# Moving a step's convolution taps ahead of the state sums in the periods that also project B and C

## The chip, the cores and the metric

The kernel runs on one core of one Trainium2 chip. The metric is the time of one execution on the device in microseconds (us); the time given for a kernel is the median of several runs. The core has engines that run side by side, each with its own queue of instructions: TensorE (PE in the profile, with its weight loads as PEld), VectorE (DVE), ScalarE (ACT), GpSimd (POOL) and SyncE (SP, which here issues the DMAs). An engine works its queue in the order in which the program issued it.

## The reference, cut to what matters

The reference is two layers on an input of 2 x 512 x 512: a feed-forward block with 4-bit weights, a state-space block (Mamba-2), the feed-forward block again, then a memory block, an attention block and the memory block again. The change is in the state-space block only. Cut to what matters there (128 heads of 64, 8 groups with a state of 128, chunks of 128 positions):

```python
proj = einsum('bsd,od->bso', h, in_proj_w)          # gate, hBC, dt
hBC = silu(causal_conv(hBC, conv_w, conv_b))         # 4 taps along the sequence
hid, B, C = split(hBC)
dt = softplus(dt + dt_bias); A = -exp(A_log)
M = einsum('bcihn,bcjhn->bcijh', Ch, Bh) * L         # L: decay inside a chunk
Y_diag = einsum('bcijh,bcjhp->bcihp', M, hc)         # hc = hid * dt
states = einsum('bclhn,bhcl,bclhp->bchpn', Bh, decay_states, hc)
prev_states = recurrence(states)                     # over the 4 chunks
Y_off = einsum('bclhn,bchpn,bhcl->bclhp', Ch, prev_states, exp(A_cs))
y = Y_diag + Y_off + Dp * hid
yg = y * silu(gate)
out = residual + group_rms_norm(yg) @ out_proj_w.T
```

## The kernel before, in words

The state-space block is `Kernel.ssm`, from L523. Its work is cut into 128 steps: for each of 8 groups, for each of 2 batches, 8 pairs of heads (`PAIRS`). One step handles one tile of 128 channels (two heads) over the 512 positions of a batch. The loop calls `period(n)` (L837) for n from 0 to 129, and each period works on three steps at once: `cur` (step n) gets its projections, its decay matrices and its convolution; `p1` (step n-1) gets its states and its output `y`; `p2` (step n-2) is multiplied with the output weights and added up.

The whole loop runs under a manual schedule: each engine gets its instructions in exactly the order in which `period` issues them. A tile that is written on one engine and read on another brings a wait. PSUM, the memory that TensorE writes to, is cut into eight banks (L528): "tr" 1, "po" 4, "dd" 1, "mm" 1 and "y" 1. Each name but "po" has a single buffer, so the next tile of that name waits until all readers of the last one are done.

In a period TensorE does, in this order: the projection of the step's channels `cp_h` (bank "dd", L715); the state matmuls `st` of p1 (bank "tr", L908); the output product `po` of p2 (L832); the two parts of `py` of p1 (bank "y"), first those from the decay matrices M (L989), then those from the states (L998); the gate projection `pg` (bank "mm"); and the transposes `ht` of the convolved channels `hid` (bank "tr", L1042).

VectorE does: `hc` and the gate's silu `v` for p1; two scans that build the decay matrices M of cur (`within`, L795; the scan is L806); the state sums `st` of p1 over the chunks (L918); the step's own taps, three per convolution (`conv_taps`, L727, the taps are L729); the product of M with CB (`times_c`, L814, L820); `hid` (the silu, L738); and `yg` of p1 (L1005, L1009).

ScalarE does: the Tanh of the gate (L849); six scalings `hd` that feed the state matmuls (L861); the Exp of the first M (L811); the first tap of the convolution, out of PSUM into `acc` (`first_tap`, L720, L724); the copy of the first chunk's state out of PSUM (L913), on which the state sums wait; the Exp of the second M (L955); and the Tanh at the end of `conv_taps` (L734).

Two periods out of eight carry more. When q is 5 (`PAIRS - 3`) the B of the next batch or group is projected, when q is 6 its C, unless there is no next one. That makes 30 periods of the 128. `group_b` and `group_c` (L767, L770) put the projection on TensorE right behind `cp_h`, into the "mm" bank (the one that `pg` takes later in the period), and append three functions to the list `late`: the first tap on ScalarE, the taps (VectorE, then a Tanh on ScalarE) and the silu at the end. `period` calls them at three places: the first tap after the state copy, the taps after the step's own taps, and the silu after `yg`. In the C periods the transposes `bt` (L777) and their copy `Btok` (L779) come as well, in the bank "tr". In periods 1 to 7 the setup of the second batch's decays (`setup_later`, L694) is spread over the period, also in the bank "tr".

Of the kernel before, what the change touches and what calls it, by code (L numbers as in the profile page):

```python
# [77 lines left out]
class Kernel:  # L78
# [758 lines left out]
    def period(self, n):  # L837
# [4 lines left out]
        late = []  # L842
# [24 lines left out]
        if cur is not None:  # L867
            g, b, q = cur.g, cur.b, cur.q
            sh = self.sh[g, b]
            for ot in (OT_HID + cur.ct, cur.ct):  # L870
                self.group_w(ot, b)
            p = self.project(self.gw[OT_HID + cur.ct], b, f"cp_h{cur.n}", "dd")
            after = cur.after()
            if after is not None and q == PAIRS - 3:
                self.group_b(*after, late)
            if after is not None and q == PAIRS - 2:
                self.group_c(*after, late)

            if n == 1:
                self.within(p1)  # L880
                nc.scalar.activation(p1.M[1], p1.M[1], AF.Exp)
                self.times_c(p1)
            if n > 0:
                self.within(cur)
            if n == 0:

                cur.pg = self.project(self.gw[cur.ct], b, f"pg{cur.n}")
                self.start(NT - 1)
            if n != 1:
                conv = self.first_tap(p, cur.ct, f"h{cur.n}")  # L890
            if n == 0:
                th = self.conv_taps(*conv)
                self.group_bt(0, 0)
                self.turn(NT - 1, "po")
                self.group_cb(0, 0, "po")
# [28 lines left out]
        if n == 1:  # L924
            conv = self.first_tap(p, cur.ct, f"h{cur.n}")
# [27 lines left out]
        if cur is not None:  # L953
            if n > 0:
                nc.scalar.activation(cur.M[1], cur.M[1], AF.Exp)  # L955
                self.setup_later(n, 1)
                th = self.conv_taps(*conv)
            for one in late:
                one[1]()
            if n > 0:  # L960
                self.times_c(cur)
            cur.hid = sp.tile([P, S], F32, tag="hid", name=f"hid{cur.n}", bufs=2)
            self.silu(cur.hid, th, conv[2])
# [817 lines left out]
```

## Time and profile before

| what | value |
|---|---|
| time, median of 3 runs | 2813.09 us |
| the three runs | 2813.09, 2822.13, 2789.83 us |
| the profiled execution, its own time | 2795.29 us |
| its span in the trace | 2793.5 us |
| its mean granted TensorE clock | 0.982 |
| busy share of PE, DVE, ACT, POOL | 96%, 73%, 39%, 19% |
| PE busy between 300 and 2300 us | 1977.6 us of 2000 |

How to read it: the profile comes from one execution, so sums are made against that execution's own time, which lies below the median. In lines of groups the fields are the line of the program, the engine, the operation, what it writes and reads (out<-in), the shapes and the count. In the timeline the first two columns are the start in us from the start of the span and the length in us of a merged run of equal instructions; a bracket at the end gives how long the engine had been idle before and what released it. In the view of waits the three numbers are the sum in us, the count and the longest. A wait labelled "issue" is one in which the profile shows nothing that the engine waited for. The ends of matmuls are modelled, and a mean over equal lines hides single ones.

### The profile page before, as it was taken

Reading aid. Unit: us, or ns where it says so; the run is one execution under the profiler, and the core shown is the slowest. Engines: PE = TensorE matmul, PEld = TensorE weight load, DVE = VectorE, ACT = ScalarE, POOL = GpSimd, SP = SyncE. Lnnn points to the kernel's source line nnn. Section 1 sums busy time; section 2 is a strip of 40 time slices with the busy share of each in tenths; the row PEclk is TensorE's granted clock in tenths of the full one; section 3 lists DMA queues with packets and bytes.
Section 4 is the critical chain, followed back from the end, with each engine's and each line's share of the span. In section 5 each row is a group of like instructions: output and inputs, shape, how many; then the busy total and the mean of one; then the engine's idle time right before and its main releaser. Section 6 shows DMA issues by size and latency. Waiting matters only on the chain.

```text
span 2793.5 us, 33412 instructions
## 1 busy us (share of the span) xinstructions
PE 2689.8 (96%) x12208; PEld 1398.5 (50%) x12208; DVE 2030.9 (73%) x3632; ACT 1102.6 (39%) x2411; POOL 522.1 (19%) x344
## 2 busy tenths in 40 slices
PE   8999999999999999999999999999999999788887
PEld 4444555555555555555555555555554444444443
DVE  7836877877888788787888878878886533555545
ACT  2214443544444344344443444434443212244442
POOL 0001131313313123132321322313230000110000
PEclk9999999999999999999999999999999999889996
DMA  7623133223223322322322332232121020000000
GB/s 209 198 89 113 72 107 128 87 91 123 96 83 124 113 72 103 129 87 80 126 105 83 121 105 80 106 128 87 68 99 46 27 84 1 0 1 1 1 1 31
DMA packets 75621, 237.77 MB, mean 85 GB/s; under 512 B 9825, under 2 KB 10401, under 8 KB 58945
## 3 DMA queue, kind: packets, MB, share of 16 engines
q1 hardware_dynamic: 70416, 226.00, 23.2%
q10 hardware_dynamic: 4752, 8.65, 0.8%
q8 instruction: 97, 1.59, 0.2%
q0 software_dynamic: 288, 0.98, 0.1%
q14 instruction: 68, 0.55, 0.1%
HBM read 223.80 MB, written 11.80 MB: 84 GB/s over the span
## 4 chain that ended last, share of the span: by engine, by line
PE 85%; DVE 9%; ACT 4%; issue 1%; DMA 0%; ACTq 0%; SPq 0%; DVEq 0%
PE pg L715 15%; PE po L832 14%; PE cp_h L715 14%; PE fo L501 5%; PE fmm L334 5%; PE py L989 4%; PE st L908 3%; PE fy L334 2%; DVE acc_h L729 2%; PE py L998 2%; PE cp_BT L715 2%; PE cp_CT L715 2%; PE ht L1042 2%; PE w L1553 1%; PE pqk L1425 1%; PE fdd L334 1%
## 5 line engine op out<-in xcount | busy, mean ns | idle before, releaser
L715 PE MATMUL pg<-hT_s,wi 128*128 128x512 f32 x1024 | 472.5, 604 | 14.4 <-issue 6.9
L832 PE MATMUL po<-wo,yg 128*128 128x512 f32 x1024 | 460.7, 593 | 0.5 <-DVE yg L1009 0.5
L715 PE MATMUL cp_h<-hT_s,wi 128*128 128x512 f32 x1024 | 460.6, 592 | 0.0
L806 DVE TENSOR_TENSOR_SCAN M<-rows,later 128x512 f32<-128x512 f32 x256 | 457.8, 1827 | 0.0
L1016 POOL TENSOR_TENSOR ssum<-ssum,sq 128x512 f32<-128x512 f32 x112 | 142.2, 1270 | 1233.0 <-ACT sq L1015 1233.0
L715 PEld LDWEIGHTS pg<-hT_s,wi 128*128 128x128 f32 x1024 | 184.2, 189 | 221.6 <-issue 213.4
L729 DVE SCALAR_TENSOR_TENSOR acc_h<-cp_h,small,acc_h 128x511 f32<-128x511 f32 (+2 forms) x384 | 286.1, 745 | 9.0
L832 PEld LDWEIGHTS po<-wo,yg 128*128 128x128 f32 x1024 | 184.8, 190 | 184.4 <-issue 183.6
L715 PEld LDWEIGHTS cp_h<-hT_s,wi 128*128 128x128 f32 x1024 | 184.6, 190 | 183.6 <-issue 183.6
L822 POOL TENSOR_TENSOR Cs<-CT,rows 128x768 f32<-128x768 f32 x128 | 251.9, 1968 | 17.6 <-PE py L998 15.7
L918 DVE SCALAR_TENSOR_TENSOR st<-st,whole,st 128x64 f32<-128x64 f32 x512 | 108.8, 274 | 125.7 <-ACT st L913 125.7
L734 ACT ACTIVATE th_h<-acc_h 128x512 f32<-128x512 f32 x128 | 80.5, 629 | 292.2 <-DVE acc_h L729 286.5
L861 ACT ACTIVATE hd<-ht,end 128x64 f32<-128x64 f32 x768 | 170.4, 323 | 35.8 <-DVE hc L853 35.7
L1015 ACT ACTIVATE sq<-yg 128x512 f32<-128x512 f32 x112 | 70.6, 630 | 286.9 <-DVE yg L1009 286.9
L820 DVE TENSOR_TENSOR M<-M,CB 128x512 f32<-128x512 f32 x256 | 164.4, 683 | 0.1
L811 ACT ACTIVATE M<-M 128x512 f32<-128x512 f32 x128 | 80.7, 630 | 199.1 <-DVE M L806 199.1
L853 DVE TENSOR_TENSOR hc<-ht,dt 128x512 f32<-128x512 f32 x128 | 88.0, 688 | 86.2 <-PE ht L1042 86.2
L1517 DVE CUSTOM_DVE_ANT_0 j<-s,future 128x384 f32<-128x384 f32 (+3 forms) x256 | 112.8, 486 | 48.8 <-PE s L1507 48.6
L989 PEld LDWEIGHTS py<-M,hc 128*64 128x64 f32 x2048 | 109.4, 136 | 68.2 <-issue 64.7
L989 PE MATMUL py<-M,hc 128*64 128x128 f32 x2048 | 140.5, 279 | 1.1 <-DVE M L820 1.1
L908 PEld LDWEIGHTS st<-hd,Btok 128*128 128x128 f32 x768 | 104.0, 191 | 70.0 <-issue 42.4
L738 DVE SCALAR_TENSOR_TENSOR v<-v,pg 128x512 f32<-128x512 f32 x128 | 87.4, 683 | 49.8 <-ACT v L849 47.7
(325 smaller groups left out, 3776.6 us busy)
## 6 DMA issues: line engine op xcount, KB each, us to landing
rows<-rows SPq DMA_DIRECT2D x128, 1024.0 KB, 4.7
wi<-in_w_in_dram SPq DMA_DIRECT2D x144, 256.0 KB, 3.5
wo<-in_w_out_dram SPq DMA_DIRECT2D x64, 256.0 KB, 3.1
keep<-w ACTq DMA_DIRECT2D x33, 256.0 KB, 3.5
wk<-keep SPq DMA_DIRECT2D x33, 256.0 KB, 2.7
wi<-in_q_dram SPq DMA_DIRECT2D x44, 128.0 KB, 3.1
sc<-in_s_dram SPq DMA_DIRECT2D x44, 128.0 KB, 3.2
wi<-in_q_dram SPq DMA_DIRECT2D x11, 256.0 KB, 3.3
```

The source lines that it names most:

```text
L334: nc.tensor.matmul(dst, lhsT=w[:, k, :], rhs=x[:, k, :], start=start and k == 0, stop=stop and k == 1, skip_group_check=True,)
L501: nc.tensor.matmul(po, lhsT=act[ht][:, b, c * P : (c + 1) * P], rhs=w2[ht], start=ht == 0, stop=ht == NHT - 1,)
L715: self.nc.tensor.matmul(p, lhsT=wt[:, k, :], rhs=self.hT[b][:, k, :], start=k == 0, stop=k == KD - 1)
L729: self.nc.vector.scalar_tensor_tensor(out=acc[:, s:], in0=p[:, : S - s], scalar=w[:, 3 - s : 4 - s], in1=acc[:, s:], op0=ALU.mult, op1=ALU ...
L806: self.nc.vector.tensor_tensor_scan(out=m, data0=rows[:, i, 0, :], data1=self.later, initial=0.0, op0=ALU.add, op1=ALU.mult,)
L820: self.nc.vector.tensor_tensor(out=m, in0=m, in1=sh["CB"], op=ALU.mult)
L822: self.nc.gpsimd.tensor_tensor(out=cur.Cs, in0=sh["CT"][:, P:].unsqueeze(1).to_broadcast([P, 2, S - P]), in1=cur.rows[:, :, 1, P:], op=ALU ...
L832: self.nc.tensor.matmul(self.po[c], lhsT=p2.yg[:, c * P : (c + 1) * P], rhs=self.wo[p2.ct], start=p2.q == 0, stop=p2.q == PAIRS - 1,)
L861: nc.scalar.mul(hd[:, c, ch], p1.pt[:, c, ch], self.dec["dt_end"][:, b * NC + c, h0 + i : h0 + i + 1],)
L908: nc.tensor.matmul(pst[:, c, :], lhsT=self.sh[p1.g, p1.b]["Btok"][:, c, :], rhs=hd[:, c, :], start=True, stop=True,)
L989: nc.tensor.matmul(py[ch, cs], lhsT=hc[:, c, ch], rhs=p1.M[i].rearrange("p (c t) -> p c t", c=NC)[:, c, :], start=c == 0, stop=c == 0, ski ...
L1016: nc.gpsimd.tensor_tensor(out=self.ssum, in0=self.ssum, in1=sq, op=ALU.add)
```

## The change

In the periods in which `late` holds something, the step's own taps and their Tanh (`conv_taps`) are issued right after the step's first tap, ahead of the states of p1. In all other periods from n = 1 on they stay where they were, after the Exp of the second M. For n = 0 they keep their place. No instruction is added or removed. For the queues of the engines this means, in the 30 periods: on VectorE the three taps come ahead of the state sums instead of behind them; on ScalarE their Tanh comes ahead of the state copy, of the first tap of B or C and of the Exp of the second M; the queues of TensorE, GpSimd and SyncE keep their order. `late` is filled earlier in the same period, so its content is known at the new place.

```diff
             if n != 1:
                 conv = self.first_tap(p, cur.ct, f"h{cur.n}")
+            if n == 0 or late:
+
+                th = self.conv_taps(*conv)
             if n == 0:
-                th = self.conv_taps(*conv)
                 self.group_bt(0, 0)
                 self.turn(NT - 1, "po")
                 self.group_cb(0, 0, "po")
...
             if n > 0:
                 nc.scalar.activation(cur.M[1], cur.M[1], AF.Exp)
                 self.setup_later(n, 1)
-                th = self.conv_taps(*conv)
+                if not late:
+                    th = self.conv_taps(*conv)
             for one in late:
                 one[1]()
             if n > 0:
```

## The prediction

> **What bounds the kernel now.** I read the busy table first, with the 40 slices under it.
>
> ```profile
> PE 2689.8 (96%) x12208; PEld 1398.5 (50%) x12208; DVE 2030.9 (73%) x3632; ACT 1102.6 (39%) x2411; POOL 522.1 (19%) x344
> ...
> PE   8999999999999999999999999999999999788887
> ...
> PEclk9999999999999999999999999999999999889996
> ```
>
> TensorE (PE) is full from the second slice to the 33rd, at full clock; VectorE (DVE) is not. The changed loop lies there. The busy time by stretches gives, for 300 to 2300 us, PE 1977.6 of 2000.0 us: only 22.4 us of PE idle can be won there, whatever becomes of the other engines. Next the view of the waits, for PE alone, from 280 to 2330 us:
>
> ```profile
> PE pg L715 <- issue: 6.9, 14, 0.7
> PE pg L715 <- DVE acc_BT L729: 5.1, 7, 0.7
> PE pg L715 <- DVE acc_CT L729: 2.4, 7, 0.3
> PE pd_dt_end L632 <- DVE row L651: 1.6, 1, 1.6
> ```
>
> The gate product `pg` waits 28 times, 14.4 us in all: 14 times about 0.71 us and 14 times about 0.33 us. The timeline shows that these are exactly the periods with a projection of B or C (30 in all; the first two behave otherwise). One such period, in the timeline of PE, then of DVE, then of ScalarE (ACT):
>
> ```profile
> 1026.50 3.60 PE L715 MATMUL cp_BT<-hT_s,wi 128*128 128x512 f32 x8
> 1029.93 0.83 PE L908 MATMUL st<-hd,Btok 128*128 128x128 f32 x6
> ...
> 1035.05 0.82 PE L998 MATMUL py<-Cs,st 128*64 128x128 f32 x12
> 1036.56 3.67 PE L715 MATMUL pg<-hT_s,wi 128*128 128x512 f32 x8 [0.68 <-issue]
> 1040.07 0.60 PE L1042 MATMUL ht<-masks,hid 128*128 128x128 f32 x4
> ```
>
> ```profile
> 1024.66 3.58 DVE L806 TENSOR_TENSOR_SCAN M<-rows,later 128x512 f32<-128x512 f32 x2
> 1031.15 0.85 DVE L918 SCALAR_TENSOR_TENSOR st<-st,whole,st 128x64 f32<-128x64 f32 x4 [2.92 <-ACT st L913]
> 1031.92 2.31 DVE L729 SCALAR_TENSOR_TENSOR acc_h<-cp_h,small,acc_h 128x511 f32<-128x511 f32 x3
> 1034.15 2.31 DVE L729 SCALAR_TENSOR_TENSOR acc_BT<-cp_BT,small,acc_BT 128x511 f32<-128x511 f32 x3
> ```
>
> ```profile
> 1027.69 0.76 ACT L724 ACTIVATE acc_h<-cp_h,small 128x512 f32<-128x512 f32 x1
> 1030.85 0.27 ACT L913 COPY st<-st 128x128 f32<-128x128 f32 x1 [2.40 <-PE st L908]
> 1031.02 0.78 ACT L724 ACTIVATE acc_BT<-cp_BT,small 128x512 f32<-128x512 f32 x1
> 1031.69 0.62 ACT L955 ACTIVATE M<-M 128x512 f32<-128x512 f32 x1
> 1034.33 0.63 ACT L734 ACTIVATE th_h<-acc_h 128x512 f32<-128x512 f32 x1 [2.01 <-DVE acc_h L729]
> ```
>
> Read them together. The extra projection puts the state matmuls at 1029.93, so DVE stands 2.92 us before its state sums, though the step's own taps need only `cp_h`, whose first tap ACT finished at 1028.45. The taps of B end at 1036.46 (1034.15 + 2.31), and `pg`, which shares the one "mm" bank with `cp_BT`, starts at 1036.56. PE had nothing left to do from 1035.87.
>
> **The change part by part.** Nothing is added or taken away. In 30 of 128 periods three taps (2.31 us) and one Tanh (0.63 us) go ahead of the state copy, the state sums and, in their own queues, the B or C first tap. PE, POOL and SP keep their order and issue the same.
>
> *DVE.* Scans end at 1028.24 (1024.66 + 3.58), the first tap at 1028.45. The taps now run 1028.45 to about 1030.8, in the 2.92 us that were idle.
>
> *ACT, the new wait.* The Tanh must wait for those taps: start 0.10 us after them, as before (1034.23 to 1034.33), so 1030.9 to 1031.5. Queued behind it are the state copy, the B first tap and the Exp of the second M. The copy moves from 1030.85 to 1031.5, 0.65 us later. Then the state sums start at about 1031.8 (was 1031.15) and end at 1032.65; the B first tap ends at 1032.45 (was 1031.80). Who waits for this: the state part of `py` on PE at 1035.05, which is still 2.4 us later. The Exp ends near 1033.0, and its multiplication on DVE comes after the B taps. Cost on PE: 0.
> [...]
>
> *The B taps.* They follow the state sums: 1032.6 to 1034.9, 1.5 us earlier than 1036.46. `pg` wants its bank at 1035.8 (in ordinary periods it starts 0.06 us before the modelled end of `py`). 0.9 us to spare, so the wait goes whole.
>
> *The C periods.* By the same rows one period on (scans end 1045.68, first tap 1045.89): taps to 1048.25, Tanh to 1048.98, copy to 1049.2, state sums to 1050.1, C taps to 1052.35, where `pg` wants its bank at 1053.58: 1.2 us to spare. The transposes `bt` need the "tr" bank of the state sums at 1051.48, 1.4 us after 1050.1. The second M of this period waits for its Exp behind the `Btok` copy until 1053.0, then `hid` ends at 1054.3; `ht` asks for it only at 1057.
>
> *Sum.* I take the length of the periods, `cp_h` to `cp_h`. An ordinary one has 13.28 us (1009.78 to 1023.06). A B period has 17.44 to 17.48 us, against 13.28 + 3.44 = 16.72 expected: 0.74 us on average. A C period has 17.39 us or 0.05 more, against 16.72 + 0.33 for `bt` = 17.05: 0.37 us. 14 x (0.74 + 0.37) = 15.6 us; the waits alone say 14.4, the lower bound of this term, and 15.6 also counts the lost overlap.
> In the first two such periods (320 to 356 us) the second batch's setup shares the "tr" bank. In the first, DVE's scans end only at 322.83, the sums go from 325.2 to about 327.2, level with `pd_start` on PE at 327.19: between -0.2 and +0.2, I take 0. In the second, the C taps end 2.2 us earlier, the row copy on DVE goes from 350.48 to about 349.0 (the Exp of M then holds it), and the 1.62 us of `pd_dt_end` shrink by 1.4. Bounds 0 and 1.6.
> What comes late next: PE's other waits are all below 1 us, single ones, so nothing takes the place of the wait.
> Total 15.6 + 1.4 = 17.0 us, bounds 14.4 and 22.4 (all PE idle in the loop).
>
> **Against which time.** The profiled execution took 2795.29 us (span 2793.5): 2778.3. It is one of the faster ones: the three timed runs have 2789.83, 2813.09 and 2822.13. The same 17.0 off their median gives 2796.1. A median of new runs should fall between, so I predict the middle, 2787.
>
> **Rivals.**
>
> *The wait stays, in part or whole (about 2795 by the profiled run, 2804 in the middle).* The chain taps, Tanh, copy, state sums, B taps is now serial over two engines; 0.9 us more in it, and `pg` waits as before. Each handover was 0.03 to 0.10 us in the rows, and there are four, so 0.9 us is hard to reach. What could do it is a scan that ends later, as in the first B period, where it takes the whole gain.
>
> *Slower: the states come too late.* If the Tanh holds the state copy until PE reaches the state part of `py`, PE stops there in all 30 periods. It decides from a slip of 2.4 us beyond my chain. At 1 us past that point it costs 30 x 1.0 = 30 us against 2795.3, with the gain gone: 2825. For it speaks that copy and sums now hang on DVE's scans, whose `rows` come by DMA; against it that no scan waits for rows in the trace, and that the periods repeat within 0.05 us.
>
> *Slower: the clock.* A still denser PE could be granted less. In 300 to 2300 us PE is 98.9% busy at granted clock 1.00; from 2300 to 2500, 87% busy, it is 0.88. Low clock goes with idleness here, not with density. One hundredth off in the 2000 us would be +20 us, or 2798.
> [...]
>
> *Faster by over 1% (28 us).* The PE idle of the loop, 22.4 us, does not hold it. Only the spread of the runs, 32 us between three of one kernel, can show it.
>
> **How the numbers follow.** The waits of `pg` go: 0.80, time 2787 (its own range 2768 to 2805: 22.4 off the fastest run, and 2822 less 17). The wait stays: 0.11. States late: 0.05. Clock: 0.04. Over all cases the range is 2767 to 2812: the lower end is the same fastest run less all PE idle, the upper end about the median before with nothing won. About 1% is what a measurement of this kernel tells from no change. My 17.0 us is 0.6%: within 1% has 0.75, faster by over 1% has 0.19 (the main case with a lucky spread), slower by over 1% has 0.06 (late states, or clock with the spread).
>
> **What would show it.** Right: DVE's wait before the state sums in B and C periods falls from 2.9 to about 1 us; the taps stand at once behind the scans; the state copy comes some 0.6 us later against the state matmuls; the waits of `pg` for `acc_BT` and `acc_CT` are gone; B periods last 16.7 and C periods 17.05 us; `pd_dt_end` waits below 0.4 us. Wrong: a wait of the state part of `py` on PE; `pg` still waiting; a granted clock below 1.00 in the loop; or ordinary periods that are no longer 13.28 us.

## The result, and the profile after

| | before | after |
|---|---|---|
| median, 21 runs each | 2807.76 us | 2792.72 us |
| lowest and highest | 2788.80 and 2822.13 us | 2778.38 and 2804.40 us |
| ratio | | 0.9955, 95% interval 0.9937 to 0.9972 |
| span of the profiled execution | 2793.5 us | 2783.0 us |

The change makes the kernel faster by 15 us, about 0.5%, with an interval that lies below 1. The page of the profile after shows that `pg` no longer waits (0.0 in its row), that VectorE's wait for the state copy fell by about half over the loop (125.7 us on the page of before, 65.5 here), and that the taps now have a wait of their own, for their first tap:

```profile
PE 2697.1 (97%) x12208; PEld 1400.7 (50%) x12208; DVE 2008.5 (72%) x3632; ACT 1105.4 (40%) x2411; POOL 522.4 (19%) x344
...
L715 PE MATMUL pg<-hT_s,wi 128*128 128x512 f32 x1024 | 473.3, 605 | 0.0
...
L806 DVE TENSOR_TENSOR_SCAN M<-rows,later 128x512 f32<-128x512 f32 x256 | 431.3, 1724 | 0.0
...
L729 DVE SCALAR_TENSOR_TENSOR acc_h<-cp_h,small,acc_h 128x511 f32<-128x511 f32 (+2 forms) x384 | 286.5, 746 | 21.3 <-ACT acc_h L724 12.3
...
L920 DVE SCALAR_TENSOR_TENSOR st<-st,whole,st 128x64 f32<-128x64 f32 x512 | 108.9, 274 | 65.5 <-ACT st L915 65.5
```

In the waits of PE from 280 to 2330 us, the three lines for `pg` are gone. What is left are single waits, those of the second batch's setup and those of the work behind the loop; two of the first kind:

```profile
PE rt L646 <- ACT z L634: 0.6, 1, 0.6
...
PE pd_dt_end L632 <- DVE row L651: 0.3, 1, 0.3
```

The same B period as in the prediction, in the timelines of PE, VectorE and ScalarE:

```profile
1018.32 3.60 PE L715 MATMUL cp_BT<-hT_s,wi 128*128 128x512 f32 x8
1021.75 0.83 PE L910 MATMUL st<-hd,Btok 128*128 128x128 f32 x6
...
1026.87 0.82 PE L1001 MATMUL py<-Cs,st 128*64 128x128 f32 x12
1027.63 3.70 PE L715 MATMUL pg<-hT_s,wi 128*128 128x512 f32 x8
```

```profile
1020.21 2.32 DVE L729 SCALAR_TENSOR_TENSOR acc_h<-cp_h,small,acc_h 128x511 f32<-128x511 f32 x3 [0.25 <-ACT acc_h L724]
1023.44 0.86 DVE L920 SCALAR_TENSOR_TENSOR st<-st,whole,st 128x64 f32<-128x64 f32 x4 [0.91 <-ACT st L915]
1024.21 2.31 DVE L729 SCALAR_TENSOR_TENSOR acc_BT<-cp_BT,small,acc_BT 128x511 f32<-128x511 f32 x3
```

```profile
1022.62 0.63 ACT L734 ACTIVATE th_h<-acc_h 128x512 f32<-128x512 f32 x1 [2.44 <-DVE acc_h L729]
1023.16 0.25 ACT L915 COPY st<-st 128x128 f32<-128x128 f32 x1
1023.30 0.78 ACT L724 ACTIVATE acc_BT<-cp_BT,small 128x512 f32<-128x512 f32 x1
```

The taps of B end at 1026.52, 1.1 us before `pg` starts, and `pg` starts where `py` leaves off. VectorE still stands 0.91 us before the state sums, because the copy now comes behind the Tanh: the state matmuls end at 1022.58, but the Tanh, which stood 2.44 us for its taps, goes first, and the copy starts at 1023.16; the sums end at 1024.30, 2.6 us before PE wants them. This is one of the B periods in which the Tanh does hold the copy. In every second B period VectorE's scans end earlier, and there, as in all C periods, the copy comes 0.87 us behind the start of the state matmuls and waits for PE alone.

Where the time went is seen when the span is cut at the first B projection that shares its periods with the second batch's setup, and at the first product after the loop. These are the busy times by stretch, in this order for before and after; the columns are the stretch, its length, the busy time of each engine, the granted clock and the DMA share:

```profile
0.00:319.65 319.65, 304.94 (x925) 148.33 (x926) 220.16 (x421) 98.97 (x196) 23.93 (x21) 0.99 0.44 143
319.65:2126.82 1807.17, 1786.36 (x8232) 956.06 (x8231) 1462.22 (x2147) 793.87 (x1852) 468.07 (x292) 1.00 0.28 100
2126.82:2793.50 666.68, 598.49 (x3052) 294.14 (x3052) 348.48 (x1066) 209.72 (x364) 30.12 (x32) 0.93 0.05 17
```

```profile
0.00:318.46 318.46, 302.96 (x926) 146.46 (x927) 219.81 (x421) 98.94 (x196) 23.94 (x21) 1.00 0.45 143
318.46:2108.72 1790.26, 1785.30 (x8232) 956.14 (x8230) 1439.54 (x2147) 796.66 (x1853) 468.37 (x292) 1.00 0.29 101
2108.72:2783.00 674.28, 608.88 (x3052) 298.12 (x3052) 349.17 (x1066) 209.80 (x364) 30.08 (x32) 0.91 0.05 16
```

The loop, from here on "the stretch", became 16.9 us shorter (1807.17 to 1790.26), with PE idle down from 20.8 to 5.0 us. What follows it has the same instructions in both and took 7.6 us longer at a granted clock of 0.91 instead of 0.93. I take that for spread between executions, not for the change: among executions with the same mean clock of 0.976, eight of before (from the runs beside the first experiments) have spans of 2805.9 to 2809.1 us (mean 2807.4) and five of after 2789.4 to 2793.2 us (mean 2791.3), a difference of 16.1 us. So the stretch, in which the clock is 1.00 in both, is the measure for the experiments, and the median of many runs is the check on it.

### The profile page after: what moved, and what is told of

The parts are those of the page before. It is cut to its first block, busy times and chain, and to the rows that moved or that the text cites. A ratio compares the mean times of both kernels' runs of the same rounds, so it can differ in the third digit from the quotient of the medians.

```text
span 2783.0 us, 33381 instructions
## 1 busy us (share of the span) xinstructions
PE 2697.1 (97%) x12208; PEld 1400.7 (50%) x12208; DVE 2008.5 (72%) x3632; ACT 1105.4 (40%) x2411; POOL 522.4 (19%) x344
## 4 chain that ended last, share of the span: by engine, by line
PE 87%; DVE 8%; ACT 4%; issue 1%; DMA 0%; SPq 0%; ACTq 0%; DVEq 0%
PE po L832 15%; PE pg L715 14%; PE cp_h L715 13%; PE fo L501 5%; PE fmm L334 5%; PE py L992 4%; PE st L910 3%; PE py L1001 3%; PE fy L334 2%; PE cp_CT L715 2%; PE cp_BT L715 2%; PE ht L1045 2%; PE w L1556 2%; DVE acc_h L729 1%; PE s L1510 1%; PE av L1572 1%
## 5 line engine op out<-in xcount | busy, mean ns | idle before, releaser
L806 DVE TENSOR_TENSOR_SCAN M<-rows,later 128x512 f32<-128x512 f32 x256 | 431.3, 1724 | 0.0
L920 DVE SCALAR_TENSOR_TENSOR st<-st,whole,st 128x64 f32<-128x64 f32 x512 | 108.9, 274 | 65.5 <-ACT st L915 65.5
```

What stands on the lines that cost most here:

```text
L806: self.nc.vector.tensor_tensor_scan(out=m, data0=rows[:, i, 0, :], data1=self.later, initial=0.0, op0=ALU.add, op1=ALU.mult,)
```

## The experiments

My theory: the gate product `pg` waits in B and C periods because it shares the one "mm" bank with the B or C projection, whose last reader is the third tap on VectorE; anything that makes that tap end before PE reaches `pg`, or takes the bank out of the question, wins the same 17 us, and nothing more is to be won there. Rivals: the gain comes from VectorE's idle time being filled, or VectorE's load going down, wherever that happens; the Tanh ahead of the state copy costs a part of it.

The table has the stretch and the mean length of each kind of period, from the start of one `cp_h` to the next in the timeline of PE, both from the one profiled execution of each kernel. The means are over the 14 groups of eight periods that begin with n = 8 and end before n = 120. The periods are named by q; 5 is a B period, 6 a C period; period 7 has the product CB and period 1 the group's norm (`pr`), both in the bank "tr". Ratios are to the kernel before, from medians of several runs.

| kernel | stretch, us | q 0 | 1 | 2 | 3 | 4 | 5 (B) | 6 (C) | 7 | ratio, 95% interval |
|---|---|---|---|---|---|---|---|---|---|---|
| before | 1807.2 | 13.43 | 14.07 | 13.48 | 13.37 | 13.29 | 17.47 | 17.41 | 14.18 | |
| after | 1790.3 | 13.43 | 14.07 | 13.50 | 13.36 | 13.29 | 16.72 | 17.05 | 14.17 | 0.9955, 0.9937 to 0.9972 |
| B periods only | 1796.5 | 13.43 | 14.07 | 13.48 | 13.37 | 13.29 | 16.72 | 17.41 | 14.18 | 0.9956, 0.9932 to 0.9981 |
| C periods only | 1801.0 | 13.43 | 14.07 | 13.49 | 13.37 | 13.29 | 17.47 | 17.05 | 14.18 | 0.9983, 0.9953 to 1.0013 |
| banks exchanged, order of before | 1852.7 | 13.43 | 14.07 | 13.48 | 13.37 | 14.93 | 18.98 | 17.39 | 14.18 | 1.0173, 1.0140 to 1.0206 |
| banks exchanged, order of after | 1838.4 | 13.43 | 14.07 | 13.50 | 13.36 | 14.91 | 18.36 | 17.15 | 14.18 | 1.0103, 1.0068 to 1.0138 |
| banks change roles, order of before | 1791.8 | 13.43 | 14.07 | 13.48 | 13.37 | 13.29 | 16.72 | 17.05 | 14.18 | 0.9941, 0.9916 to 0.9966 |
| banks change roles, order of after | 1790.3 | 13.43 | 14.07 | 13.50 | 13.36 | 13.29 | 16.72 | 17.05 | 14.17 | 0.9958, 0.9929 to 0.9988 |
| Tanh left behind | 1789.4 | 13.43 | 14.07 | 13.48 | 13.37 | 13.29 | 16.72 | 17.05 | 14.18 | 0.9917, 0.9882 to 0.9953 |
| taps ahead in every period | 1865.6 | 13.29 | 16.44 | 14.19 | 13.57 | 13.56 | 16.72 | 17.05 | 15.41 | 1.0189, 1.0115 to 1.0264 |
| the same, Tanh left behind | 1800.5 | 13.29 | 14.28 | 13.84 | 13.29 | 13.29 | 16.72 | 17.05 | 14.45 | 0.9985, 0.9952 to 1.0018 |
| two extra operations | 1792.7 | 13.43 | 14.07 | 13.50 | 13.36 | 13.29 | 16.80 | 17.05 | 14.18 | 0.9922, 0.9886 to 0.9958 |
| four extra operations | 1828.5 | 13.43 | 14.07 | 13.50 | 13.36 | 13.29 | 17.77 | 18.36 | 14.17 | 1.0034, 0.9999 to 1.0069 |

### One half of the change alone

```diff
-            if n == 0 or late:
+            ahead = n == 0 or (late and q == PAIRS - 3)
+            if ahead:
                 th = self.conv_taps(*conv)
...
-                if not late:
+                if not ahead:
                     th = self.conv_taps(*conv)
```

The diff is that for the B periods; for the C periods it has `PAIRS - 2`.

B periods only. 

> The changed order in the B periods only; C periods as before. Measure: the stretch from the first B projection of the loop with both setups (step 5) to the first product after the loop, 1807.2 us before and 1790.3 us after. Theory (the gate product waits for the mm bank, each period by itself): B periods at 16.71 us, C periods at 17.4 us, 14 x 0.74 + 0.4 = 10.8 us less, 1796.4 us. Rival (the gain comes from VectorE being less busy or less held up over the whole loop, by any such move alike): half, 8.5 us less, 1798.7 us, with C periods shorter too.

C periods only. 

> The changed order in the C periods only. Theory: C periods at 17.05 us, B periods still 17.46 us, and the 1.3 us of the decay's wait in step 6: 14 x 0.37 + 1.3 = 6.5 us less, stretch 1800.7 us. Rival (any move alike): 8.5 us less, 1798.7 us.

Measured 1796.5 and 1801.0 us, both within 0.3 us of the theory. Each kind of period takes its new length exactly where the order was changed and keeps the old one elsewhere. The two gains, 10.7 and 6.2 us, add up to the 16.9 of the whole. The rival of a gain shared by all periods alike falls. It falls by the stretch alone: the ratios of the two halves, 0.9956 and 0.9983, and of the whole, 0.9955, have intervals that overlap.

### The banks exchanged

```diff
+            own, other = "dd", "mm"
+            if after is not None and q in (PAIRS - 3, PAIRS - 2):
+                own, other = other, own
-            p = self.project(self.gw[OT_HID + cur.ct], b, f"cp_h{cur.n}", "dd")
+            p = self.project(self.gw[OT_HID + cur.ct], b, f"cp_h{cur.n}", own)
...
-                self.group_b(*after, late)
+                self.group_b(*after, late, other)
...
-                self.group_c(*after, late)
+                self.group_c(*after, late, other)
```

In the order of before. 

> The kernel before with no instruction moved; only the two PSUM banks change places in the B and C periods: the step's own projection goes to mm, that of B or C to dd. Theory (the bank alone makes the wait): the gate product then waits for the step's own taps, which end 2.2 us earlier than those of B or C, so its waits go in full, 14 x (0.74 + 0.37) = 15.5 us less, stretch 1791.6 us; VectorE still stands 2.9 us before the state sums. Rival (VectorE's idle time filled is what brings the gain): nothing gained, 1807.2 us.

In the order of after. 

> The kernel after, with the two banks also exchanged. Theory: no bank wait is left to remove, stretch 1790.3 us within 0.5, ratio to before as that of after. Rival (two independent gains that add up): 1775 us.

Both came out slower than before, 1852.7 and 1838.4 us, and both expectations failed. The waits of `pg` did go, but `cp_h` got a new one, shown by the timeline of PE with the banks exchanged in the order of before:

```profile
1044.88 3.70 PE L715 MATMUL cp_h<-hT_s,wi 128*128 128x512 f32 x8 [1.57 <-DVE v L738]
...
1064.16 5.40 PE L715 MATMUL cp_h<-hT_s,wi 128*128 128x512 f32 x8 [2.30 <-DVE v L738]
```

I had looked at who uses "mm" behind `cp_h` in the period and not at who still holds it ahead of it: the gate product of the period before lies there until VectorE has done the silu `v` that reads it. `cp_BT` comes 3.4 us later in the period and never met that reader; `cp_h` is the first thing PE does, and does. Period 4 (in whose length the wait of the next `cp_h` lies) grew by 1.64 us and period 5 by 1.51, period 6 shrank by 0.26, to 17.15, if two of the 14 are left out that a lower clock made 1.7 us longer (last section): 2.89 us for each pair of B and C, 14 times 40.5 of the 45.5 us, and 3.4 more for those two. So this edit traded one bank wait for another, and did not decide between the theories.

### The banks change roles

To take out the wait of `pg` without a new one, `pg` goes to the bank of the step's own projection, and the names change roles afterwards, so that each projection finds a bank whose last reader is long done. Every instruction stays where before had it.

```diff
+            self.roles = "dd", "mm"
             for n in range(len(self.steps) + 2):
                 self.period(n)
...
+            own, other = self.roles
-            p = self.project(self.gw[OT_HID + cur.ct], b, f"cp_h{cur.n}", "dd")
+            p = self.project(self.gw[OT_HID + cur.ct], b, f"cp_h{cur.n}", own)
...
-                self.group_b(*after, late)
+                self.group_b(*after, late, other)
...
-                self.group_c(*after, late)
+                self.group_c(*after, late, other)
...
-                cur.pg = self.project(self.gw[cur.ct], b, f"pg{cur.n}")
+                cur.pg = self.project(
+                    self.gw[cur.ct], b, f"pg{cur.n}", own if late else other
+                )
+            if late:
+                self.roles = other, own
```

In the order of before. 

> The kernel before with every instruction at its old place. In B and C periods the gate product goes to the bank of the step's own projection, and the banks dd and mm then change roles for the periods that follow, so that no bank is asked for while the gate's silu still reads it (that was the new wait in the run that exchanged the banks). Theory (the bank alone makes the wait): the gate product's waits go, cp_h gets none, B periods 16.72 us and C periods 17.05 us, stretch 14 x 1.11 = 15.5 us less, 1791.7 us; VectorE still stands 2.9 us before the state sums. Rival (VectorE's idle time has to be filled): B periods stay at 17.47 us, stretch 1807.2 us.

In the order of after. 

> The kernel after with the same change of roles of the two banks. Theory: one wait, removed twice; stretch 1790.3 us within 0.5, periods as after. Rival (two separate gains): 1774.7 us.

Measured 1791.8 and 1790.3 us, 0.1 us or less from the theory. In the order of before, with nothing moved, B periods fall to 16.72 us while VectorE stands as long as ever before its state sums (timeline of VectorE, then of PE):

```profile
1023.99 0.86 DVE L920 SCALAR_TENSOR_TENSOR st<-st,whole,st 128x64 f32<-128x64 f32 x4 [2.89 <-ACT st L915]
1024.76 2.31 DVE L730 SCALAR_TENSOR_TENSOR acc_h<-cp_h,small,acc_h 128x511 f32<-128x511 f32 x3
1026.99 2.31 DVE L730 SCALAR_TENSOR_TENSOR acc_BT<-cp_BT,small,acc_BT 128x511 f32<-128x511 f32 x3
```

```profile
1027.89 0.82 PE L1000 MATMUL py<-Cs,st 128*64 128x128 f32 x12
1028.64 3.70 PE L716 MATMUL pg<-hT_s,wi 128*128 128x512 f32 x8
```

The taps of B end at 1029.30, after `pg` has begun, and nobody waits. All 28 waits of `pg` are gone from the view of the waits, also the 14 that it labelled "issue". So the idle time of VectorE had no price of its own; the bank had. Nor had VectorE's load: its scans take 461.6 us in all here, against 457.8 before and 431.3 after, and the periods are as short as after. The change and the exchange of roles are two cures of one wait: together they bring no more than one. This also shows that the 1.5 us by which the change is ahead (1790.3 against 1791.8) come from the first pair of periods, where the decay's wait is not one for "mm".

### The Tanh left behind

```diff
-    def conv_taps(self, p, w, acc, name):
+    def conv_taps(self, p, w, acc, name, end=True):
...
+        return self.conv_end(acc, name) if end else None
+
+    def conv_end(self, acc, name):
         th = self.early.tile([P, S], F32, tag="th", name=f"th_{name}", bufs=2)
...
-            if n == 0 or late:
+            ahead = n == 0 or late
+            if ahead:
-                th = self.conv_taps(*conv)
+                th = self.conv_taps(*conv, n == 0)
...
-                if not late:
-                    th = self.conv_taps(*conv)
+                th = self.conv_end(*conv[2:]) if ahead else self.conv_taps(*conv)
```

> The kernel after, in B and C periods only, with the Tanh left at its old place behind the Exp on ScalarE. Theory (the 0.65 us by which the Tanh delays the state copy are covered): stretch 1790.3 us within 1 us, state copy 0.6 us earlier on ScalarE, no other change. Rival (the Tanh ahead of the copy costs part of the gain): 30 x 0.6 = up to 18 us less, 1772 us.

Measured 1789.4 us, 0.9 us less than after, 0.84 of it in the first B period of the stretch: there VectorE is late, the copy then waits only for PE, and the Exp of the setup comes 1.0 us earlier. All later B and C periods are equal to 0.02 us. So in the first B period the Tanh ahead of the copy has a price, 0.84 us. The 0.5 to 0.6 us by which it delays the copy in every second one of the other B periods are covered. The ratio of 0.9917 is not distinguishable from that of after, as their intervals overlap; by the stretch this is the shortest of all kernels here, by a margin far below what the runs can resolve.

### Taps ahead in every period

```diff
-            if n == 0 or late:
+            ahead = n != 1
+            if ahead:
                 th = self.conv_taps(*conv)
...
-                if not late:
+                if not ahead:
                     th = self.conv_taps(*conv)
```

The run with the Tanh left behind takes the diff of the section before, with this `ahead`.

With the Tanh. 

> The kernel after, with taps and Tanh ahead of the states in every period but two, the ordinary ones too. Theory (the Tanh holds up the state copy, and the state part of the output product then waits on TensorE; in ordinary periods that margin is not there): state sums end near 1.4 us after TensorE wants them, in some 97 periods, +136 us: stretch 1926 us, ordinary periods 14.7 us. Rival (the copy passes, or the order on VectorE and ScalarE is covered everywhere): 1790 us.

With the Tanh left behind. 

> As the run with every period, but only the three taps go ahead; the Tanh stays behind the state copy and the Exp on ScalarE. Theory (the Tanh in ScalarE's queue makes most of the lateness, the taps on VectorE the rest): state sums end 0.4 us after TensorE wants them, 97 x 0.4 = 39 us: stretch 1829 us. Rival (the taps on VectorE make all of it): 1926 us, as with the Tanh.

Measured 1865.6 and 1800.5 us: slower than after by 75.4 and 10.3 us. The direction and the share of the two queues were right, since most of the loss goes with the Tanh; the sizes, 136 and 39, were not. In plain periods such as q 4 the state sums end only 0.3 us too late instead of 1.4. The timeline of PE shows the large losses elsewhere, in periods 1 and 7:

```profile
1044.25 1.11 PE L1001 MATMUL py<-Cs,st 128*64 128x128 f32 x12
...
1091.73 1.13 PE L786 MATMUL cb<-CT,BT 128*128 128x128 f32 x8 [1.00 <-DVE st L920]
...
1120.87 1.02 PE L940 MATMUL pr<-masks,ssum 128*128 128x1 f32 x8 [1.44 <-DVE st L920]
```

Three things were missing in my sum. First, the taps moved ahead let `hid` and `yg` end earlier, so the next period's work on VectorE starts earlier: in period 4 the scans end 4.84 us after `cp_h` starts in every group, while before they end 4.5 and 5.8 us after it by turns. Second, `pr` and `cb` ask for the bank "tr", which the state sums hold, before PE reaches the state part of `py`; with late sums they wait first (period 1 is 2.37 us longer on average, period 7 1.24). Third, the clock: behind eight of the stops the matmuls slowed down, with a granted clock of 0.50 in the one shown in the last section, and of the 14 periods in the mean of period 1 the six in which this happened last 17.3 to 17.7 us, the others 15.6 to 15.8; from the start of `pr` to the next `cp_h` it is 8.2 against 6.6 us. By that difference, 1.6 us, an estimate for the eight is 13 of the 75.4 us. That the condition `late` limits the change to the periods with a spare 3.4 us of PE work ahead of the states is what keeps it a gain.

### Extra work on VectorE

```diff
+            if late:
+                for _ in range(2):
+                    nc.vector.tensor_tensor(
+                        out=self.later, in0=self.later, in1=self.later, op=ALU.max
+                    )
             if n == 0 or late:
```

The run with four has `range(4)`.

Two operations. 

> As the run with four extra operations, with two (1.28 us). Theory: the taps of B end 1.0 us later, which the 1.1 us to spare still cover; stretch 1790.3 us, at most 2 us more. Rival (all VectorE time counts): 30 x 1.28 = 38 us more, 1829 us.

Four operations. 

> The kernel after, with four extra VectorE operations of 0.69 us (2.5 us in a row, idempotent) ahead of the taps in the B and C periods. Theory (1.1 us to spare in B periods, 1.9 us in C periods, then every us counts; 0.25 us of the extra work is free, the taps waited for their first tap): the taps of B end 2.25 us later, the gate product waits 1.15 to 1.2 us in B and 0.3 us in C periods, 14 x 1.5 = 21 us more, stretch 1811 us. Rival (the order no longer matters, VectorE is not the bound): 1790 us. Rival (all VectorE time counts): 30 x 2.5 = 75 us more, 1865 us.

Two cost 2.4 us over 30 periods, just beyond the 2 expected, so VectorE time of 38 us was nearly all absorbed, as the theory has it. Four cost 38.2 us, beyond the 21 expected: 5.1 of it in the first pair of periods, the rest in the others, 1.05 us for a B and 1.31 us for a C period, where 0.3 was expected for C. The timeline of PE with four shows a wait of `pg` in the B period and one of `bt` in the C period:

```profile
1048.60 3.67 PE L715 MATMUL pg<-hT_s,wi 128*128 128x512 f32 x8 [1.49 <-issue]
...
1064.77 0.52 PE L777 MATMUL bt<-masks,BT 128*128 128x128 f32 x3 [1.09 <-DVE st L925]
```

In C periods the bank "tr" became the limit ahead of "mm": the transposes `bt` wait for the state sums, which end at 1064.63. I had named that margin in the prediction and left it out of this expectation. Also, the scans that take 2.74 us in the C period of the kernel after are back at 3.58 us here (the last section shows what the 2.74 ran beside), which eats another 0.8 us of the margin. As long as the last reader of each bank was done in time, next to nothing was lost here (2.4 us with two operations, of 38 us of VectorE time); with four operations, beyond the margins, the two waits shown are 1.49 and 1.09 us.

## Why the prediction was right, point by point

- *The wait goes whole in B and C periods.* Right: 17.47 to 16.72 and 17.41 to 17.05 us, 0.75 and 0.36 for the 0.74 and 0.37 forecast; 14 times that is 15.5 us, and so it is with the forecast figures, which the prediction's sum puts at 15.6. That the bank is the cause is shown by the change of roles.
- *The first pair.* Near in both: the first B period became 0.2 us shorter (19.02 to 18.81) where I took 0 with bounds of 0.2 to either side, the first C period 1.3 us (20.82 to 19.52) for 1.4. The wait of `pd_dt_end` went from 1.6 to 0.3. That the stretch comes out within 0.1 us of 17.0 is luck in part, since the small excess makes up for small shortfalls.
- *The Tanh's wait costs nothing on PE.* Right in the 28 periods, but the wait itself is rarer than I forecast. In the B period shown the copy comes 1.41 us behind the start of the state matmuls instead of 0.92, so 0.49 later rather than 0.65, and the sums end 2.6 us before they are wanted, for 2.4 forecast. That is so in every second B period (1.41 to 1.52 us); in the others and in all C periods the copy stays at 0.87, because the scans end early enough for the Tanh to be out of the way. In the first B period the Tanh did cost PE 0.84 us, as the run with the Tanh left behind shows.
- *The margins.* The taps of B end 1.1 us early, for 0.9; those of C at 1042.72, 1.95 us before `pg`, for 1.2, because the scans there became shorter. The second M does wait for its Exp, 0.82 us in the timeline of VectorE; the forecast named the wait and left next to nothing for it. `hid` still ends 2.8 us before `ht`, for 2.7.
- *The rivals.* "The wait stays" and "the states come too late" both exist as mechanisms: the four extra operations bring the first back, the taps in every period show the second, though mostly by way of the bank "tr". Neither comes near in this change. The clock in the loop stayed at 1.00.
- *The time.* 2792.7 for 2787. The step of 17.0 us held in the stretch (16.9) and was 15.0 between the medians. What I set too low was the starting point: I took the middle of the profiled execution and the median of three, 2804, while more runs put the median before at 2807.8.
- *Not foreseen:* VectorE's scans, from 1827 to 1724 ns each. They took 26 us less in all (457.8 to 431.3), and that changed no time in the loop: with the banks' roles changed the scans took 461.6 us and the periods were as short.

## What to carry to other kernels

A short wait that repeats in the same place on a full engine is worth following to the last reader of the buffer it asks for; here it was 0.3 to 0.7 us, 28 times, from one bank with two users. It could be cured on either side, by letting the reader finish earlier (1790.3 us) or by giving the waiting product another bank (1791.8), and the second needs no new order, provided that one also looks at who holds that bank from the period before. Work moved ahead in a queue was free here only where the engine that wants what now comes later had other work to do first: the same move that wins 17 us in 30 periods ends 58 us behind the kernel before when made in all of them (1865.6 against 1807.2 us).

## What the runs showed of the hardware

*Scans slow down beside GpSimd.* Both timelines of the kernel after, VectorE's scans first and then GpSimd's product `Cs`:

```profile
1016.38 3.59 DVE L806 TENSOR_TENSOR_SCAN M<-rows,later 128x512 f32<-128x512 f32 x2
...
1033.00 2.74 DVE L806 TENSOR_TENSOR_SCAN M<-rows,later 128x512 f32<-128x512 f32 x2
```

```profile
1015.95 1.82 POOL L822 TENSOR_TENSOR Cs<-CT,rows 128x768 f32<-128x768 f32 x1
...
1031.74 1.81 POOL L822 TENSOR_TENSOR Cs<-CT,rows 128x768 f32<-128x768 f32 x1
```

The first pair of scans shares 1.39 us with `Cs` and takes 3.59 us, the second shares 0.55 us and takes 2.74. Over the loop, pairs that share nothing take 2.33 us, about 1.0 us shared gives 3.15 and 1.7 us gives 3.91: nearly a us lost for each us shared. Pairs that run beside a `Cs` which itself took 2.73 us instead of 1.81 last 3.7 to 4.9 us, so the count does not hold there. In the period after B, `Cs` now starts 0.14 us after `cp_h` (1031.74 and 1031.60) where it was 1.17 us before (1041.67 and 1040.50), so it is nearly over when the scans begin. That this is why the scans became shorter is read from the traces and was not tried by itself.

*Behind some short stops of PE the clock was halved.* With the banks exchanged in the order of before, `cp_h` waited 2.3 us seven times from 420 us on, and twice the product behind it took 5.40 us instead of 3.70, as in the line above that starts at 1064.16. The busy times by stretch of that kernel give the granted clock, the third column from the end, in the second us after the stop (0.67) and in the third (0.50):

```profile
1064.10:1065.10 1.00, 0.94 (x2) 0.49 (x3) 1.00 (x2) 0.51 (x3) 1.00 (x1) 1.00 0.00 0
1065.10:1066.10 1.00, 1.00 (x3) 0.53 (x2) 1.00 (x1) 0.00 (x0) 0.30 (x1) 0.67 0.00 0
1066.10:1067.10 1.00, 1.00 (x2) 0.34 (x1) 1.00 (x2) 0.59 (x1) 0.00 (x0) 0.50 0.00 0
```

The 21 stops of 1.7 us or less in the same part were not followed by it. In another kernel shorter stops were. With the taps ahead in every period the matmuls behind a stop slowed down eight times in the stretch. Seven times this began within 2.3 us of the end of a stop ahead of `pr`, stops of 1.4 to 1.7 us (the eighth came behind one of 1.84 us ahead of `cb`); behind the eight other stops ahead of `pr`, 1.25 to 1.44 us, the matmuls kept their times. One of the seven, in the timeline of PE, followed by the busy times in the second us behind the stop, with the granted clock at 0.50:

```profile
518.96 1.02 PE L940 MATMUL pr<-masks,ssum 128*128 128x1 f32 x8 [1.42 <-DVE st L920]
519.91 1.98 PE L992 MATMUL py<-M,hc 128*64 128x128 f32 x16
```

```profile
520.00:521.00 1.00, 1.00 (x10) 1.00 (x12) 0.68 (x2) 0.96 (x2) 0.00 (x0) 0.50 0.00 0
```

The same `py` took 1.10 us behind an equal stop of 1.42 us one group later (640.65). So stops of 2.3 us were followed by a halved clock in two of seven cases ahead of `cp_h`, and stops of 1.25 to 1.7 us by slower matmuls in seven of fifteen ahead of `pr`, while none of the 21 of 1.38 to 1.69 us ahead of `cp_h` was. Why some stops and not others was not shown.
